# Cross-attention on one core: 25 key chunks of 128 and two keys in a resident sample, in place of 26 chunks of about 123

## The chip, the core and the metric

The kernel runs on one core of a Trainium2 chip. A core has TensorE (matrix products, with weight loads listed apart), VectorE, ScalarE and GpSimd (elementwise work and reductions), and SyncE, which here only issues DMA transfers. The metric is the device time of one execution in microseconds (us).

## The reference

All numbers are 32-bit floats. 4096 query rows x and 3202 context rows, each 512 wide, are layer-normalized. Eight heads of 64 attend from the queries to the context; the result is projected, added to x, normalized again, and fed to a small recurrence of 64 states. Cut to what matters here:

```python
x = layernorm(builder_state, g1, beta1)          # 4096 x 512
base_n = layernorm(base_state, g1, beta1)        # 3202 x 512
q, k, v = heads(x, Wq, bq), heads(base_n, Wk, bk), heads(base_n, Wv, bv)
attn = softmax(q @ k.T / sqrt(64))               # 8 heads, 4096 x 3202
x = residual + (attn @ v) @ W_o.T + b_o
U = (layernorm(x, g2, beta2) @ W_in.T + b_in) @ Bmat
# s = silu(s @ A.T) + u_t over 4096 steps; out = x + states @ Cmat + mod
```

## The kernel before

*Preparation* (up to `prep.close()`, L586). The 3202 context rows are split into `NCH` = 26 chunks of 122 to 124 rows (`keys(c)`, L50; `key0(c)`, L56, is where a chunk begins). A chunk is loaded (`load_chunk`), normalized (`norm_chunk`: statistics on VectorE, factors on GpSimd, scaling on ScalarE) and transposed (`turn_chunk`). Its values are four products into `pv` (L542), copied on ScalarE to `vs` and stored to `vd` in DRAM (L552). After every fourth chunk, and after the last, the keys of that group of chunks are projected for each of four pairs of heads (`pk`, L568), biased on ScalarE into `ks` (L576), and stored to `kd` in DRAM (L581). Side work, such as the first queries, is threaded between. Within this part each engine takes its instructions in the order in which they are written.

*Attention.* The queries are taken in `NQB` = 8 groups of 512. A unit is one group Q, one pair of heads hp, and one half of the group (`QU` = 256 queries): 64 units. A unit goes through `NDC` = 13 steps; a step c is a pair of blocks, that is of chunks, of keys. Per step:

- `scores` (L615): for two blocks b, two halves of a block's keys and two heads a, a product with 256 moving columns. Contraction is over the 64 values of a head, so each product uses one quarter (64 by 64) of TensorE's array, and the four of one block use all quarters. In the trace a product of 32-bit floats is two instructions, so a step's scores are 16.
- `weights` (L670): ScalarE takes the exponential of the step's scores, 1024 a partition, less a shift.
- `product` (L694): the exponentials times the values, again quarter by quarter, 16 instructions, summed over the unit in PSUM (`po`).
- `add` (L678): the exponentials are summed elementwise into `acc`, on VectorE, in steps 2, 6 and 10 on GpSimd (`POOL_SUMS`). At a unit's end GpSimd folds the two blocks (`fold`, L683) and TensorE sums over the keys (`sums`, L708) for the denominator, which ScalarE copies out (L734) into `rd` and a scratch tile.

The shift is common to the two halves of a (Q, hp). Before its first unit a *sample* of scores is made (`sample`, L632): the first 64 keys of block 0, from the loaded tile `kts[Q, hp, 0]`, with all 512 queries. VectorE takes the maximum (`maximum`, L644), TensorE spreads it (`spread`, L651), and VectorE reduces it to the shift (`base`, L662). The sample lies in one of the two PSUM buffers that scores use (ring `s`).

Keys and values of a step are loaded from DRAM by `load_k` (L953) and `load_v` (L961), issued on SyncE's queue 10 and 6 steps ahead of the scores that they are for, once for both halves of a (Q, hp) except in the last group of queries.

*What sets the order.* The class `Plan` (L60) is a planner: each piece of work is given an engine, an assumed cost in ns, the pieces it comes after, a due time, and rings of buffers that it takes or gives back. `order()` runs a list schedule with these costs, earliest due first, and the pieces are then emitted in that order, which is fixed for each engine. Products are due `LAG` = 4 steps after their scores. Kinds of pieces in quarters and of whole-array pieces are kept together, as a change between them is assumed to cost time. The pieces of a unit are added in `unit` (L1302), those of its end in `finish` (L725).

*The end.* `drain` (L1358) adds the recurrence in two sweeps over 16 rows in parallel columns, the last query rows, and the output. A general version of the attention (`attend`, L1458) runs only where checks on the device find that the quick one doesn't hold.

Of the kernel before, what the change touches and what calls it, by code (L numbers as in the profile page):

```python
# [20 lines left out]
P = 128  # L21
NC = H // P
NCH = 26
CK = 124
NDC = NCH // 2
GC = 4
# [15 lines left out]

RISE = 2.0**60
# [6 lines left out]
def keys(c):  # L50


    return {0: CK, 1: CK, 2: CK - 2, NDC - 1: CK}.get(c // 2, CK - 1)


def key0(c):  # L56
    return sum(keys(k) for k in range(c))
# [104 lines left out]
def xattn_ssm_kernel(  # L162
# [41 lines left out]
    shifts = const.tile([P, NQB * NC], F32, name="shifts")  # L204
    neg_half = const.tile([P, 1], F32, name="neg_half")
# [308 lines left out]
    with tc.manual_schedule():  # L514
# [20 lines left out]
        for c in range(NCH):  # L535
# [5 lines left out]
            for i in range(NC):  # L541
# [8 lines left out]
            vs = cin.tile([CK, NC, P], F32, tag="vs", name=f"vs_{c}")  # L550
            nc.scalar.copy(vs[:n], pv[:n, :H])
            nc.sync.dma_start(  # L552
                vd[:, c // 2, :n, c % 2, :].rearrange("h p d -> p h d"), vs[:n]
            )
# [10 lines left out]
            for hp in range(NC):  # L565
# [13 lines left out]
                for b in range(g * GC, c + 1, 2):  # L579
                    m, k = 2 * keys(b), key0(b) - key0(g * GC)  # L580
# [26 lines left out]
    def scores(w, c):  # L607

        n, q = keys(2 * c), w["q"]
        s = ps_s.tile([P, 2, 2, QU], F32, tag="s", name=f"s_{w['name']}_{c}")  # L610
        for b in range(2):
            for k0, k1 in ((0, HD), (HD, n)):
                for a in range(2):
                    r = slice(a * HD, (a + 1) * HD)
                    nc.tensor.matmul(  # L615
                        s[k0:k1, a, b, :],
                        kts[(*w["at"][:2], c)][r, b * n + k0 : b * n + k1],
# [7 lines left out]
    def sample(w):  # L625
# [3 lines left out]
        for part in range(2):  # L629
            for a in range(2):  # L630
                r = slice(a * HD, (a + 1) * HD)
                nc.tensor.matmul(  # L632
                    s[part * HD : (part + 1) * HD, a, 0, :],
                    kts[Q, hp, 0][r, :HD],
                    qt[Q, hp][r, part * QU : (part + 1) * QU],
# [29 lines left out]

    def weights(w, c):

        n = keys(2 * c)
        t = w["s"][c] = sp_.tile([CK, 2, 2, QU], F32, tag="s", name=f"p_{w['name']}_{c}")
        nc.scalar.activation(t[:n], w["ps"][c][:n], AF.Exp, bias=w["shift"][:n])  # L670

    def add(w, c, engine):

        n, t = keys(2 * c), w["s"][c]
# [3 lines left out]
        engine.tensor_tensor(w["acc"][:n], t[:n], before[:n], ALU.add)  # L678
# [6 lines left out]
    def product(w, c):  # L685


        n, t = keys(2 * c), w["s"][c]
        if c == 0:
            w["po"] = ps_o.tile([P, 2, 2 * QU], F32, tag="o", name=f"po_{w['name']}")  # L690
        for b in range(2):
            for a in range(2):
                for k, (k0, k1) in enumerate(((0, HD), (HD, n))):
                    nc.tensor.matmul(  # L694
                        w["po"][a * HD : (a + 1) * HD, k, :QU],
                        vts[(*w["at"][:2], c)][k0:k1, b, a * HD : (a + 1) * HD],
# [1004 lines left out]
```

## Time and profile before

| | us |
|---|---|
| median of the runs shown (three, 2144.7 to 2152.58) | 2149.72 |
| profiled execution, device time | 2149.4 |
| its span, first to last instruction | 2147.6 |
| TensorE busy (matmul) | 2081.9 |
| TensorE busy (weight loads, beside the matmuls) | 1528.4 |
| ScalarE busy | 1245.4 |
| VectorE busy | 1086.0 |
| GpSimd busy | 759.9 |
| mean granted clock of TensorE, share of full | 0.990 |

In the views of the profile PE is TensorE's matmuls, PEld its weight loads, DVE VectorE, ACT ScalarE, POOL GpSimd, SPq SyncE's queue. A group's row gives line, engine, operation, out<-in, the shape and the count, then its busy time and the mean duration of one in ns, then the idle time of the engine just before its instructions and what ended it. Busy times count time in which at least one instruction of the group ran, so matmuls that overlap in quarters are not counted four times. A row of the chain of waits or of the timeline gives start and length in us.

### The profile page before, as it was taken

How to read it: one execution, taken by the hardware profiler on the slowest of the kernel's cores; microseconds unless marked ns; L12 is line 12 of the kernel's file. 1: busy time of each engine (PE TensorE's matmuls, PEld its weight loads, DVE VectorE, ACT ScalarE, POOL GpSimd, SP SyncE). 2: the span in 40 equal slices, each digit the busy share in tenths (PEclk: the TensorE clock that was granted, in tenths of full speed). 3: DMA queues.
4: the chain of work that ended last, by engine and by line, in shares of the span. 5: the costliest groups of instructions: out<-in, count | busy, mean ns of one | idle time of the engine just before them, and what ended most of it. 6: DMA issues, size and time to landing. Idle time of an engine off the chain costs nothing.

```text
span 2147.6 us, 67311 instructions
## 1 busy us (share of the span) xinstructions
PE 2081.9 (97%) x29822; PEld 1528.4 (71%) x29822; DVE 1086.0 (51%) x1227; ACT 1245.4 (58%) x1734; POOL 759.9 (35%) x622
## 2 busy tenths in 40 slices
PE   6998999999999999999999999999999999999997
PEld 2444587787788777887778777877787777767754
DVE  2121056555555546464556455555555464645555
ACT  2132267656665677557656676566656675566642
POOL 1111034334432444234423443344424442344313
PEclk9999999999999999999999999999999999999997
DMA  3332332222221222122212322222222221444464
GB/s 118 122 122 93 91 97 80 64 74 75 80 75 57 74 74 82 53 65 93 78 59 78 93 78 63 73 77 81 74 57 74 74 82 53 125 130 133 132 191 159
DMA packets 178117, 190.73 MB, mean 89 GB/s; under 512 B 14252, under 2 KB 151256, under 8 KB 177818
## 3 DMA queue, kind: packets, MB, share of 16 engines
q1 hardware_dynamic: 173270, 178.67, 27.4%
q10 hardware_dynamic: 4548, 7.67, 1.2%
q8 instruction: 237, 3.88, 0.8%
q14 instruction: 62, 0.51, 0.1%
HBM read 156.40 MB, written 29.89 MB: 87 GB/s over the span
## 4 chain that ended last, share of the span: by engine, by line
PE 79%; ACT 6%; DVE 5%; DMA 4%; POOL 4%; issue 1%; SPq 1%; ACTq 0%; POOLq 0%; DVEq 0%
PE s L615 29%; PE po L694 27%; PE pq L301 5%; PE pv L542 4%; PE pk L568 3%; DVE acc L678 3%; PE pa L874 3%; ACT p L670 2%; DMA x<-in_x_dram 2%; POOL acc L678 2%; PE pu L921 1%; PE pd L708 1%; POOL rstd_x L795 1%; PE tp_x L271 1%; ACT xh_x L799 1%
## 5 line engine op out<-in xcount | busy, mean ns | idle before, releaser
L670 ACT ACTIVATE p<-s,shifts 123x1024 f32<-123x1024 f32 (+2 forms) x832 | 922.3, 1115 | 371.3 <-PE s L615 368.8
L694 PE MATMUL po<-p,v 64*64 64x256 f32 (+3 forms) x13312 | 887.1, 376 | 0.2 <-DVE o L723 0.2
L615 PE MATMUL s<-q,k 64*64 64x256 f32 (+3 forms) x13312 | 885.2, 377 | 0.8 <-ACT p L670 0.2
L678 DVE TENSOR_TENSOR acc<-p,acc 123x1024 f32<-123x1024 f32 (+2 forms) x515 | 644.2, 1251 | 447.1 <-POOL acc L678 230.3
L678 POOL TENSOR_TENSOR acc<-p,acc 122x1024 f32<-122x1024 f32 x189 | 447.2, 2366 | 851.4 <-ACT p L670 496.1
L694 PEld LDWEIGHTS po<-p,v 64*64 64x64 f32 (+3 forms) x13312 | 586.1, 133 | 137.9 <-issue 13.0
L615 PEld LDWEIGHTS s<-q,k 64*64 64x64 f32 (+3 forms) x13312 | 571.0, 131 | 157.3 <-issue 15.6
L678 DVE TENSOR_TENSOR acc<-p,p 124x1024 f32<-124x1024 f32 x64 | 86.0, 1343 | 147.7 <-ACT p L670 147.7
L683 POOL TENSOR_TENSOR acc<-acc 124x512 f32<-124x512 f32 x64 | 81.5, 1274 | 132.2 <-DVE acc L678 109.4
L301 PE MATMUL pq<-xn,wq 128*128 128x256 f32 x512 | 117.4, 384 | 0.0
L742 DVE RECIPROCAL rd<-rd 128x256 f32<-128x256 f32 (+1 forms) x65 | 111.7, 1720 | 0.4
L301 PEld LDWEIGHTS pq<-xn,wq 128*128 128x128 f32 x512 | 95.2, 190 | 21.7 <-issue 9.7
L874 PE MATMUL pa<-wo,o 128*128 128x512 f32 x240 | 108.8, 601 | 0.0
L542 PE MATMUL pv<-wv,ct 128*123 128x512 f32 (+2 forms) x208 | 99.9, 626 | 0.0
L568 PE MATMUL pk<-ct,wk 128*128 128x492 f32 (+3 forms) x224 | 89.1, 550 | 0.0
L576 ACT ACTIVATE ks<-pk,bias 128x492 f32<-128x492 f32 (+3 forms) x28 | 18.0, 642 | 118.8 <-PE pk L568 59.8
L723 DVE TENSOR_TENSOR o<-po,o 128x256 f32<-128x256 f32 x64 | 26.9, 420 | 112.7 <-ACT o L719 112.5
L874 PEld LDWEIGHTS pa<-wo,o 128*128 128x128 f32 x240 | 43.7, 190 | 51.3 <-issue 50.8
L310 ACT ACTIVATE q<-pq,bias 128x512 f32<-128x512 f32 x32 | 22.0, 686 | 95.8 <-PE pq L301 95.8
L782 ACT ACTIVATE xh_y<-x 128x512 f32<-128x512 f32 x30 | 18.8, 627 | 98.3 <-DVE x L884 98.3
L512 DVE COPY ct<-tp_c 128x492 f32<-128x492 f32 (+2 forms) x13 | 8.7, 671 | 126.3 <-PE tp_c L271 126.3
L542 PEld LDWEIGHTS pv<-wv,ct 128*123 128x123 f32 (+2 forms) x208 | 39.3, 197 | 46.7 <-issue 45.8
(190 smaller groups left out, 1308.0 us busy)
## 6 DMA issues: line engine op xcount, KB each, us to landing
k<-kd SPq DMA_DIRECT2D x324, 123.0 KB
v<-vd SPq DMA_DIRECT2D x324, 123.0 KB
k<-kd SPq DMA_DIRECT2D x108, 124.0 KB
v<-vd SPq DMA_DIRECT2D x108, 124.0 KB
xr<-in_x_dram SPq DMA_DIRECT2D x32, 256.0 KB
x1d<-xr SPq DMA_DIRECT2D x32, 256.0 KB
x<-in_x_dram SPq DMA_DIRECT2D x28, 256.0 KB
cx<-in_ctx_dram SPq DMA_DIRECT2D x18, 246.0 KB
```

The costliest lines, as they stand in the source:

```text
L301: nc.tensor.matmul(pq[:, half * QU : (half + 1) * QU], wq[:, i, hp * P : (hp + 1) * P], xns[half][:, i, :], start=(i == 0), stop=(i == NC ...
L310: nc.scalar.activation(t, pq, AF.Identity, bias=bias[:, hp : hp + 1], scale=HD**-0.5)
L542: nc.tensor.matmul(pv[:n, :H], ct[:, i, o : o + n], wv[:, i, :], start=(i == 0), stop=(i == NC - 1),)
L568: nc.tensor.matmul(pk[:, :n_g], wk[:, i, hp * P : (hp + 1) * P], ct[:, i, :n_g], start=(i == 0), stop=(i == NC - 1),)
L615: nc.tensor.matmul(s[k0:k1, a, b, :], kts[(*w["at"][:2], c)][r, b * n + k0 : b * n + k1], q[r], start=True, stop=True, skip_group_check=True,)
L670: nc.scalar.activation(t[:n], w["ps"][c][:n], AF.Exp, bias=w["shift"][:n])
L678: engine.tensor_tensor(w["acc"][:n], t[:n], before[:n], ALU.add)
L683: nc.gpsimd.tensor_tensor(acc[:, :, 0, :], acc[:, :, 0, :], acc[:, :, 1, :], ALU.add)
L694: nc.tensor.matmul(w["po"][a * HD : (a + 1) * HD, k, :QU], vts[(*w["at"][:2], c)][k0:k1, b, a * HD : (a + 1) * HD], t[k0:k1, a, b, :], sta ...
L723: nc.vector.tensor_tensor(o, w["po"][:, 1, :QU], o, ALU.add)
L742: nc.vector.reciprocal(w["rd"][:, part], w["rd"][:, part])
L874: nc.tensor.matmul(v["pa"], o_t[Q, c, t // 2][:, t % 2 * P : (t % 2 + 1) * P], wo[:, c, :], start=(c == 0), stop=(c == NC - 1),)
```

## The change

The 3202 keys become 25 full chunks of 128 (`CK` = 128) and a 26th chunk of the two keys that are left (`REST` = 2).

- In the preparation the 26th chunk's values go to `vx`, an SBUF tile that is zero elsewhere, on partitions 0 and 1, and by a small DMA also on partitions 64 and 65. GpSimd copies keys into `kx`, 64 for each pair of heads: the two keys left over first, then the first 62 keys. `vd` gets no values of the 26th chunk.
- Step 12 of a unit has one block: scores, weights, products and addition are of half size there.
- The sample is made from `kx`, so its scores hold those of the two keys left over. A new piece `extra` on ScalarE takes the exponential of all the sample's scores, once the shift is known, into a tile of a ring of 4; it gives back the sample's PSUM buffer, which `base` gave back before. Sample columns are ordered so that query half t of each unit stands on partitions t * 64 on.
- `rest`, a new piece on VectorE, adds the two keys' exponentials to `acc` in each unit: two additions on two partitions and 2 x 128 columns, after the unit's addition 1 and before 2.
- Ahead of step 12's products come four products of 128 columns, exponentials of the sample times `vx`, into `po`. As `vx` is zero elsewhere, only the two keys count.
- The sample no longer waits for the step of the unit before that issued its keys' load.
- The copy of the second denominator goes back to its own PSUM tile, not to a scratch tile.
- The planner's costs are given anew: scores 864 (before 860) and 432 for the half step, products 864 and 650, weights 1061 and 630, additions on VectorE 1300 and 700, `extra` 640, `rest` 700.

```diff
-CK = 124
+CK = 128
+REST = S2 - (NCH - 1) * CK
 def keys(c):
-    return {0: CK, 1: CK, 2: CK - 2, NDC - 1: CK}.get(c // 2, CK - 1)
+    return CK if c < NCH - 1 else REST
+def blocks(c):
+    return 2 if c < NDC - 1 else 1
...
+    kx = const.tile([P, NC, HD], F32, name="kx")
+    vx = const.tile([P, H], F32, name="vx")
+    nc.gpsimd.memset(vx, 0.0)
...
+            if c < NCH - 1:
+                vs = cin.tile([CK, NC, P], F32, tag="vs", name=f"vs_{c}")
+                nc.scalar.copy(vs, pv)
+                nc.sync.dma_start(vd[:, c // 2, :, c % 2, :].rearrange("h p d -> p h d"), vs)
+            else:
+                nc.scalar.copy(vx[:n], pv[:n])
+                nc.sync.dma_start(vx[HD : HD + n], vx[:n])
...
+                if g == 0:
+                    nc.gpsimd.tensor_copy(kx[:, hp, REST:], ks[:, : HD - REST])
+                elif c == NCH - 1:
+                    nc.gpsimd.tensor_copy(kx[:, hp, :REST], ks[:, CK : CK + REST])
...
     def scores(w, c):
-        for b in range(2):
-            for k0, k1 in ((0, HD), (HD, n)):
+        for b in range(blocks(c)):
+            for k0 in (0, HD):
...
     def sample(w):
-        for part in range(2):
+        q = qt[Q, hp].rearrange("p (h t j) -> p t h j", h=2, t=2)
+        for t in range(2):
             for a in range(2):
                 nc.tensor.matmul(
-                    s[part * HD : (part + 1) * HD, a, 0, :],
-                    kts[Q, hp, 0][r, :HD],
-                    qt[Q, hp][r, part * QU : (part + 1) * QU],
+                    s[t * HD : (t + 1) * HD, a, 0, :],
+                    kx[r, hp, :],
+                    q[r, t],
...
+    def extra(w):
+        t = extras[w["at"][:2]] = accp.tile([P, 2, 2, P], F32, tag="extra", name=f"x_{w['name']}", bufs=4)
+        nc.scalar.activation(
+            t, w["sample"][:, :, 0, :].rearrange("p a (h j) -> p a h j", h=2), AF.Exp, bias=w["shift"]
+        )
+
+    def rest(w):
+        t = extras[w["at"][:2]][:, :, w["at"][2], :]
+        for k in range(2):
+            r, to = slice(k * HD, k * HD + REST), w["acc"][:, :, 0, k * P : (k + 1) * P]
+            nc.vector.tensor_tensor(to[r], t[r], to[r], ALU.add)
...
     def product(w, c):
+        if c == NDC - 1:
+            for a in range(2):
+                for k in range(2):
+                    r = slice(k * HD, (k + 1) * HD)
+                    nc.tensor.matmul(
+                        w["po"][a * HD : (a + 1) * HD, k, k * P : (k + 1) * P],
+                        vx[r, hp * P + a * HD : hp * P + (a + 1) * HD],
+                        extras[Q, hp][r, a, half, :],
+                        start=False, stop=False, skip_group_check=True,
+                    )
-        for b in range(2):
+        for b in range(blocks(c)):
...
-            to = w["rd"] if k == 0 else op.tile([P, QU], F32, tag="junk", ...)
+            to = w["pd"][k][:, :QU] if k else w["rd"]
...
-            free = [("scores", i - 1, NDC - AHEAD_K)] if i else []
-            plan.add(("sample", i), "PE", 440, partial(sample, w), q + free, d, ["s"], ...)
-            plan.add(("base", i), "DVE", 280, partial(base, w), [("spread", i)], d + 1000, [],
+            plan.add(("sample", i), "PE", 440, partial(sample, w), q, d, ["s"], ...)
+            plan.add(("base", i), "DVE", 280, partial(base, w), [("spread", i)], d + 1000)
+            plan.add(("extra", i), "ACT", 640, partial(extra, w), [("base", i)], d + 1000, ["extra"],
                      [("s", ("sample", i))])
...
+            if c == 1:
+                plan.add(("rest", i), "DVE", 700, partial(rest, w), [("add", i, 1), ("extra", first)],
+                         d + 1300, [], [("extra", ("extra", first))])
```

Left out above: the loads of `load_k` and `load_v`, which take one block in step 12; the additions, which take half there; the planner's other costs; and `attend`, which follows the new layout.

More of the change, by code (lines that the diff above doesn't have):

```diff
@@ L50, in keys @@
 def keys(c):
-    return {0: CK, 1: CK, 2: CK - 2, NDC - 1: CK}.get(c // 2, CK - 1)
+    return CK if c < NCH - 1 else REST
+def blocks(c):
+    return 2 if c < NDC - 1 else 1
 def key0(c):
-    return sum(keys(k) for k in range(c))
+    return c * CK
 class Plan:
@@ L677, in add @@
             w["acc"] = accp.tile([CK, 2, 2, QU], F32, tag="acc", name=f"acc_{w['name']}")
-        engine.tensor_tensor(w["acc"][:n], t[:n], before[:n], ALU.add)
+        engine.tensor_tensor(
+            w["acc"][:, :, :nb, :], t[:, :, :nb, :], before[:, :, :nb, :], ALU.add
+        )
     def fold(w):
@@ L706, in sums @@
         for a in range(2):
[L707 removed]
+            for k, (k0, k1) in enumerate(((0, HD), (HD, P))):
                 nc.tensor.matmul(
@@ L732, in denominators @@
                 w["rd"] = op.tile([P, QU], F32, tag="rd", name=f"rd_{name}", bufs=2)
-            to = w["rd"] if k == 0 else op.tile([P, QU], F32, tag="junk", name=f"junk_{name}", bufs=1)
+            to = w["pd"][k][:, :QU] if k else w["rd"]
             nc.scalar.activation(
@@ L951, in load_k @@
             t = kp.tile([P, 2 * CK], F32, tag="k", name=f"k_{Q}_{hp}_{half}_{c}")
-            n = 2 * keys(2 * c)
+            n = blocks(c) * CK
             nc.sync.dma_start(t[:, :n], kd[hp, c, :, :n])
@@ L1323, in unit @@
             d = max(s0 - REF, 0) * STEP
-            free = [("scores", i - 1, NDC - AHEAD_K)] if i else []
-            plan.add(("sample", i), "PE", 440, partial(sample, w), q + free, d, ["s"],
+            plan.add(("sample", i), "PE", 440, partial(sample, w), q, d, ["s"],
                      [("q", ("heads", Q, hp))], "quarters")
@@ L1336, in unit @@
             old = [("product", *divmod(g, NDC))] if g >= 0 else []
-            plan.add(("scores", i, c), "PE", 860, partial(scores_, c), q + old, d, ["s"],
+            part = blocks(c) / 2
+            plan.add(("scores", i, c), "PE", 864 * part, partial(scores_, c), q + old, d, ["s"],
                      [("q", ("heads", Q, hp))], "quarters")
-            plan.add(("weights", i, c), "ACT", 1061, partial(weights, w, c),
+            plan.add(("weights", i, c), "ACT", 200 + 861 * part, partial(weights, w, c),
                      [("scores", i, c), ("base", first)], d + 1000, ["p"],
@@ L1343, in unit @@
             p = ("p", ("weights", i, c))
-            plan.add(("product", i, c), "PE", 860, partial(product_, c),
-                     [("weights", i, c)] + ([("product", i, c - 1)] if c else []),
-                     d + 1000, [] if c else ["o"], [p], "quarters")
+            more, gives = [], [p]
+            if c == NDC - 1:
+                more, gives = [("extra", first)], [p, ("extra", ("extra", first))]
+            plan.add(("product", i, c), "PE", 864 if part == 1 else 650, partial(product_, c),
+                     [("weights", i, c)] + ([("product", i, c - 1)] if c else []) + more,
+                     d + 1000, [] if c else ["o"], gives, "quarters")
             if c:
                 dve = w["last"] or c not in POOL_SUMS
-                plan.add(("add", i, c), "DVE" if dve else "POOL", 1300 if dve else 2382,
+                before = {1: ("weights", i, 0), 2: ("rest", i)}.get(c, ("add", i, c - 1))
+                plan.add(("add", i, c), "DVE" if dve else "POOL", (100 + 1200 * part) if dve else 2382,
                          partial(add, w, c, nc.vector if dve else nc.gpsimd),
-                         [("weights", i, c), ("weights" if c == 1 else "add", i, c - 1)], d + 1200,
+                         [("weights", i, c), before], d + 1200,
                          ["acc"] if c == 1 else [],
                          [p] + ([("p", ("weights", i, 0))] if c == 1 else []))
+            if c == 1:
+                plan.add(("rest", i), "DVE", 700, partial(rest, w), [("add", i, 1), ("extra", first)],
+                         d + 1300, [], [("extra", ("extra", first))])
         d += 2000
```

84 lines of the change are left out of this document (44 added, 40 removed).

## The prediction

> **What bounds the kernel now.** I read the page first, then the busy time by stage, then the chain of waits inside one stretch of the loop, then what TensorE itself waited for. The page:
>
> ```profile
> span 2147.6 us, 67311 instructions
> PE 2081.9 (97%) x29822; PEld 1528.4 (71%) x29822; DVE 1086.0 (51%) x1227; ACT 1245.4 (58%) x1734; POOL 759.9 (35%) x622
> ...
> L615 PE MATMUL s<-q,k 64*64 64x256 f32 (+3 forms) x13312 | 885.2, 377 | 0.8 <-ACT p L670 0.2
> ```
>
> No engine but TensorE is near its limit, yet a busy PE need not be a PE at its peak, so the stages come next (columns: stretch, length, busy time and instructions of each engine, granted clock, DMA):
>
> ```profile
> 0.00:259.20 259.20, 226.40 (x661) 107.40 (x661) 46.71 (x110) 64.84 (x103) 33.14 (x98) 0.98 0.34 107
> 259.20:2063.00 1803.80, 1791.18 (x28857) 1381.46 (x28858) 997.47 (x993) 1159.83 (x1561) 700.94 (x489) 1.00 0.28 82
> 2063.00:2147.60 84.60, 64.33 (x308) 39.51 (x306) 41.85 (x125) 20.69 (x71) 25.85 (x36) 0.81 0.55 170
> ```
>
> The attention loop is 1803.8 of 2147.6 us, and TensorE is busy for 1791.2 of it at a granted clock of 1.00. Whether that time is also full is seen in a stretch of pure loop, and in the chain of waits around one sample:
>
> ```profile
> 709.94:728.93 18.99, 18.99 (x356) 16.07 (x352) 13.31 (x12) 12.42 (x13) 7.88 (x4) 1.00 0.12 31
> ```
>
> ```profile
> 458.80 0.86 PE po L694 x16
> 459.67 0.43 PE sm L632 x8
> 460.10 0.87 PE po L694 x16
> 460.97 0.86 PE s L615 x16
> 461.83 0.84 PE po L694 x15
> 462.67 0.09 PE sm L651 x5
> 462.75 0.05 PE po L694
> 462.80 0.01 PE sm L651
> 462.81 0.86 PE po L694 x14
> 463.68 1.73 PE s L615 x32
> ```
>
> In 18.99 us the sequencer issued 352 weight loads, each with its matmul: 22 pieces of 16 (the scores or the products of one pair of blocks), 0.863 us a piece. The chain steps from one piece to the next with no gap and no other engine between them. The waits of TensorE over the loop (waiter, releaser, us, times, longest) say the same, and those of ScalarE say who leads:
>
> ```profile
> PEld s L615 <- ACT p L670: 12.5, 32, 0.6
> PE tp_x L271 <- ACT xh_x L799: 10.4, 16, 1.2
> ```
>
> ```profile
> ACT p L670 <- PE s L615: 368.8, 555, 2.0
> ```
>
> ScalarE waits 369 us for scores, TensorE hardly ever for anything. So the loop goes at the rate at which TensorE can issue, and matmul time taken out of it comes off the end, unless something new stalls it.
>
> **The change, part by part.** The loop has 64 units (8 groups of 512 queries, 4 pairs of heads, 2 halves) of 13 steps. The diff makes step 12 one block instead of two.
>
> *Matmuls removed.* Their cost follows the moving columns, 256 queries, and not the keys: the page's group holds forms with 58, 59, 60 and 64 keys, and keys set only the stationary side, so blocks of 128 keys cost what blocks of 123 did. That half a piece costs half shows at the sample: eight instructions of 256 columns, 0.43 us. Per unit half of a scores piece and half of a products piece go: 2 x 0.4315 = 0.863 us; over 64 units 55.2 us.
>
> *Matmuls added.* Four products of 128 columns per unit, eight instructions over the four quadrants. No row has this form. By columns they cost half of the sample's 0.43, 0.216 us. The nearest rows on both sides are the sample (0.43) and the spreading of the maximum just after it, eight instructions of 64 columns, 0.09 + 0.05 + 0.01 = 0.15 us with a product between. I take 0.216, since the short row shows that one instruction per 19 ns can go through and mine need only one per 27 ns: 64 x 0.216 = 13.8 us, bounds 9.6 and 27.5.
>
> A rule of the Trainium skill speaks against this. TensorE: Matmul & The Clock Gate, Back-to-back issue gap, states that in a stream of weight loads and matmuls a matmul of 128 columns takes about 81 ns, more than its columns alone. By it 512 instructions would cost 41.5 us, an estimate, and the change would keep 13.7 us. The row of 64 columns, with 19 ns each, does not agree for quadrants that run side by side; no row here shows 128 columns in quadrants.
>
> *The sample moves.* It multiplies the resident keys (two left over and the first 62) with the same 512 queries in eight instructions: 0.43 us as before. What is new is that its score buffer, one of two, is given back by an exponential on ScalarE and not by the VectorE reduction before it. Here is that time in the trace:
>
> ```profile
> 461.95 1.11 ACT L670 ACTIVATE p<-s,shifts 123x1024 f32<-123x1024 f32 x1 [1.98 <-PE s L615]
> 464.60 2.12 ACT L670 ACTIVATE p<-s,shifts 123x1024 f32<-123x1024 f32 x2 [1.54 <-PE s L615]
> ```
>
> ```profile
> 462.87 0.29 DVE L662 TENSOR_REDUCE shifts<-sm 128x1 f32<-128x128 f32 x1
> ```
>
> ```profile
> 264.40 0.69 ACT L310 ACTIVATE q<-pq,bias 128x512 f32<-128x512 f32 x1 [6.20 <-PE pq L301]
> ```
>
> The reduction ends at 463.16. ScalarE is idle from 463.06 to 464.60, so an exponential of 512 elements (0.69 us by the row of that size, and some 0.15 us, an estimate, for the two hand-overs) fits there, and the buffer is free at about 464.0 and not 463.2. The chain's two scores pieces begin at 463.68 and 464.54; the first has the other buffer, freed at 463.06, and the second needs this one with half a microsecond to spare. Queued behind the exponential are the next weights; they wait for scores anyway. So the hold costs nothing where the order falls like this. Where ScalarE is in the middle of weights it may cost up to the whole 0.85 us, 32 x 0.85 = 27.2 us. Below nothing is excluded: the buffer is never held shorter. I take 0.1 us each, 3 us, near the end that the trace shows.
>
> *ScalarE and VectorE.* The rows for them, of the groups by form:
>
> ```profile
> L670 ACT ACTIVATE p<-s,shifts 123x1024 f32<-123x1024 f32 x576 | 638.6, 1115 | 269.6 <-PE s L615 267.3
> L678 DVE TENSOR_TENSOR acc<-p,acc 123x1024 f32<-123x1024 f32 x450 | 564.5, 1254 | 437.5 <-POOL acc L678 230.3 <-ACT p L670 188.4 <-POOL nm_y L796 3.4
> L678 POOL TENSOR_TENSOR acc<-p,acc 123x1024 f32<-123x1024 f32 x126 | 298.4, 2368 | 636.2 <-ACT p L670 343.4 <-DVE acc L678 292.8
> L749 DVE TENSOR_TENSOR o<-o,rd 128x256 f32<-128x256 f32 x63 | 56.9, 903 | 1.5
> L739 DVE TENSOR_TENSOR rd<-pd,rd 128x256 f32<-128x256 f32 x64 | 26.8, 420 | 8.5 <-ACT junk L734 8.5
> ```
>
> ScalarE loses about half of 64 exponentials (64 x 0.5 = 32 us) and gains 32 x 0.69 = 22: a little lighter. VectorE loses half of 64 additions (64 x 0.6 = 38 us) and gains 128 small ones on two partitions, 256 elements, between 0.42 and 0.90 us each by the last two rows: 54 to 115 us, so it stands at 1100 to 1165 us, below 56% of the span. These additions lie between the second addition of a unit and the third, on GpSimd; the whole chain of a unit is then 9 x 1.25 + 3 x 2.37 - 0.6 + 1.8 = 19.6 us at most, against 1803.8 / 64 = 28 us for a unit of the loop now, and 27.6 after. Cover enough: 0. The second denominator copy writes PSUM instead of a scratch tile, same size: 0.
>
> *DMA and queues.* Each pair of heads still issues its 13 loads of keys and 13 of values, same queue, same bytes in all (the DMA share in the loop is 0.28). The sample no longer waits for a step that issued its keys: 0.
>
> *Preparation.* There are still 26 chunks; the last holds two keys and its value products cost what a full one does. Key products follow the columns:
>
> ```profile
> 230.05 13.37 PE L568 MATMUL pk<-ct,wk 128*128 128x492 f32 x32
> ...
> 250.12 6.86 PE L568 MATMUL pk<-ct,wk 128*128 128x248 f32 x32
> ```
>
> From these, 6.5 us for 244 columns: six groups of 512 instead of some 492 add 6 x 0.53 = 3.2 us, and the last group of 130 instead of 248 saves up to 3.1 us. I take +1. GpSimd gets eight copies of up to 62 columns behind the key projections; in the first group the normalization of a later chunk queues behind one:
>
> ```profile
> 63.03 0.67 ACT L576 ACTIVATE ks<-pk,bias 128x496 f32<-128x496 f32 x1 [7.21 <-DMA kd<-ks]
> 63.60 0.80 ACT L255 ACTIVATE xh_c<-cx,nmr_c,rstd_c 123x512 f32<-123x512 f32 x1
> ...
> 70.45 0.58 PE L271 MATMUL tp_c<-ident,xh_c 123*128 123x123 f32 x4
> ```
>
> It would be some 2 us late, and the transposes that need it come at 70.45, about 6 us after its end; were that cover gone, the 2 us would be paid once. Cost 0.
>
> *Tail.* It is a serial scan with its own chain; only the last addition shrinks, by 0.6 us: 0.
>
> **Sum.** -55.2 + 13.8 + 3 + 1 = -37.4 us. The profiled execution took 2149.4 us, its span 2147.6, and the median of the runs shown is 2149.72, so both scales agree to 0.3 us. Forecast: 2149.4 - 37.4 = 2112 us, 1.7% faster.
>
> **Rivals.**
>
> *The held buffer stalls TensorE.* If the second scores piece finds the sample's buffer taken in every one of 32 samples, with no products ready to fill in, 27.2 us replace the 3: 2136 us. For it: two buffers only, and 12.5 us of waits for weights already, in 32 places. Against it: products stand four steps behind scores by the order's due times, and TensorE filled the present 3.8 us hold with them.
>
> *The short products do not overlap.* Their columns stream for only 0.216 us, and the weights of eight instructions must come in within it. One weight load takes 133 ns:
>
> ```profile
> L694 PEld LDWEIGHTS po<-p,v 64*64 64x64 f32 x6656 | 488.1, 133 | 137.9 <-issue 13.0 <-DVE o L723 2.9 <-DMA k<-kd 0.8
> ...
> 563.69 1.02 PE pu L921 x8
> ```
>
> Mild form: only two of them run at a time, 8 x 133 / 2 = 0.53 us a unit, 34.0 us instead of 13.8, and the time is 2132 us. Slow form, and the rival that ends slower: the short products, at the head of step 12's products, go one after another as the eight 128-column matmuls of the state inputs do (the second row, 1.02 us): 65.3 us instead of 13.8, and the time is 2163 us. From 0.80 us a unit on, (55.2 - 4) / 64, the change loses. Against both: eight 64-column instructions in the same four quadrants took 0.15 us, with weights of the same size. By the rule of the Trainium skill above it would be 2140 us, an estimate.
>
> *The change doesn't do what it says.* The work written for step 12 shrinks, but the order is planned anew, and a step of half length may leave TensorE waiting at each unit's end for most of the half-size exponential (0.69 us by the row above, say 0.6) with nothing else ready: 64 x 0.6 = 38 us would be given back and 2150 us remain. For it: the planner counts costs and not what really happens. Against it: the next unit's scores and products four steps behind are ready at that place, as in all of the loop now.
>
> **How the numbers follow.** Forecast 0.79; held buffer 0.10; short products 0.03 in the mild form and 0.02 in the slow one; time given back 0.06. About 0.5%, 11 us, is what a measurement of this kernel can tell from no change, so faster means below 2139 us. Forecast, held buffer and mild form are faster, 0.92, less 0.02 for a hold with a whole exponential of weights queued in front (another 1.1 us in part of the samples), which would end within 0.5%. With 0.04 of the time given back that makes 0.06 for the same; its other 0.02 and the slow form are 0.04 for slower. The range: with short products at 0.15 us and nothing for buffer and preparation the sum gives 2104; upward, short products at 0.43 give 2126, and three quarters of the held buffer's stall 2130. So 2103 to 2130.
>
> **What would show it.** In the profile after: 12800 instead of 13312 instructions in the scores' group, eight short product instructions per unit taking about 0.22 us in the chain; the loop some 38 us shorter, preparation and tail within 2 us of 259 and 85. Wrong would be the buffer's step if scores' waits for weights grow from 12.5 us by tens; the short products' step if the chain gives them 0.4 us or more; the cover on VectorE if sums or products wait for additions; the whole, if the loop loses less than 20 us.

## The result and the profile after

| | before | after |
|---|---|---|
| median, us | 2148.77 (2144.7 to 2152.58) | 2094.67 (2093.36 to 2095.41) |
| profiled execution, us | 2149.4 | 2095.41 |
| its span, us | 2147.6 | 2093.2 |

The ratio is 0.9748, with a 95% interval of 0.9729 to 0.9767: 54 us or 2.5% faster. The direction was right, but the time is 17 us below the forecast of 2112 and 8 us below the lower end of the range. The page after:

```profile
span 2093.2 us, 66347 instructions
PE 2039.0 (97%) x29310; PEld 1342.8 (64%) x29310; DVE 1102.0 (53%) x1355; ACT 1241.2 (59%) x1766; POOL 756.1 (36%) x631
...
L741 PE MATMUL po<-p,v 64*64 64x256 f32 x12800 | 838.8, 377 | 13.6 <-DVE o L770 13.6
...
L631 PE MATMUL s<-q,k 64*64 64x256 f32 x12800 | 837.2, 377 | 3.1 <-ACT p L701 1.8
```

TensorE is busy for the same 97%, so the page alone does not say where the gain came from. The busy time by stage does, if the stages hold the same work. The prediction's loop ended with the last product, and by that end it went from 1803.8 to 1776.0 us. But in the kernel after, the order that is planned anew puts the last half step's products behind output projections (`py`) and the first steps of the recurrence (`z`), over 8 us after the products ahead of them:

```profile
1998.11 4.50 PE L741 MATMUL po<-p,v 64*64 64x256 f32 x80
2002.43 0.61 PE L755 MATMUL pd<-acc,ones 64*64 64x256 f32 x8
2002.97 1.98 PE L1211 MATMUL py<-wo,o 128*128 128x512 f32 x4
...
2010.70 0.45 PE L729 MATMUL po<-x,vx 64*64 64x128 f32 x8
```

Before, the last products follow one another. So I end the loop with the last scores. To there the kernels differ by 512 matmul instructions, 1016 taken out and 504 put in. The loop and what comes behind it, before and then after (columns as in the prediction: stretch, length, PE, PEld, DVE, ACT, POOL, granted clock, DMA share, GB/s):

```profile
259.20:2057.10 1797.90, 1785.28 (x28756) 1377.02 (x28760) 995.06 (x987) 1157.65 (x1555) 697.62 (x486) 1.00 0.27 82
2057.10:2147.60 90.50, 70.23 (x413) 43.95 (x404) 44.26 (x131) 22.86 (x76) 29.17 (x38) 0.82 0.57 177
```

```profile
0.00:235.60 235.60, 221.05 (x662) 103.45 (x662) 46.02 (x110) 65.89 (x103) 34.96 (x107) 1.00 0.38 117
235.60:1998.30 1762.70, 1743.62 (x28244) 1194.53 (x28248) 1011.45 (x1115) 1152.78 (x1587) 691.80 (x487) 1.00 0.29 84
1998.30:2093.20 94.90, 74.38 (x412) 44.82 (x404) 44.55 (x131) 22.53 (x76) 29.32 (x38) 0.79 0.51 152
```

| stage | before | after | difference | forecast |
|---|---|---|---|---|
| preparation | 259.2 | 235.6 | -23.6 | +1 |
| loop, to the last scores | 1797.9 | 1762.7 | -35.2 | -38.4 |
| tail, from the last scores | 90.5 | 94.9 | +4.4 | 0 |

Two steps of the forecast failed. The preparation, where nothing was to happen, gave 23.6 of the 54 us. In the loop, TensorE's busy time fell by 41.7 us, and 41.4 were forecast for its matmuls; but its idle time rose from 12.6 to 19.1 us, and behind this stand two waits that moved in opposite directions; their rows come further down.

The tail is 85 to 90 us long in those of the sixteen kernels here that were granted a clock of 0.89 or more in it, and 90 to 96 at 0.83 or less, with nearly the same work. So I compare stages, and the loop above all. How well the loop repeats differs: in after and the two kernels below whose loop is the same it took 1762.3 to 1762.7 us; before took 1797.9 and a kernel with the same loop 1801.7. Differences of a few us are no reading between kernels of another order.

The signs that the prediction named: the scores' group has 12800 instructions, as told, and the short products take 0.22 us in the chain, as told. The chain around them:

```profile
320.53 0.22 PE po L729 x8
320.75 0.43 PE po L741 x8
```

The held sample buffer costs nothing that shows: the scores' waits for weights went from 12.5 us to 8.8. New is the second row, the wait that the prediction named as the sign against its step on VectorE; it was 0.2 us before. Gone is most of a wait that the prediction shows at 10.4 us, for the normalized queries (`xh_x`): the third row (waits of TensorE and of its weight loads: waiter, releaser, us, times, longest):

```profile
PEld s L631 <- ACT p L701: 8.8, 17, 1.2
PE po L741 <- DVE o L770: 13.6, 14, 1.7
PE tp_x L281 <- ACT xh_x L846: 1.3, 6, 0.3
```

So a wait of 13.4 us that was forecast at nothing came in, and 9.1 us that nobody counted went out. Why they went is not shown; it is luck that the loop ends within 3.2 us of its forecast.

### The profile page after: what moved, and what is told of

Same layout as the page of the kernel before. It is cut to its first block, busy times and chain, and to the rows that moved or that the text cites. A ratio compares the mean times of both kernels' runs of the same rounds, so it can differ in the third digit from the quotient of the medians.

```text
span 2093.2 us, 66347 instructions
## 1 busy us (share of the span) xinstructions
PE 2039.0 (97%) x29310; PEld 1342.8 (64%) x29310; DVE 1102.0 (53%) x1355; ACT 1241.2 (59%) x1766; POOL 756.1 (36%) x631
## 4 chain that ended last, share of the span: by engine, by line
PE 81%; DVE 7%; ACT 5%; POOL 5%; issue 2%; DMA 0%; POOLq 0%; ACTq 0%; DVEq 0%
PE po L741 27%; PE s L631 26%; PE pq L311 6%; PE pa L921 5%; PE pv L552 4%; DVE acc L709 4%; PE pk L580 4%; ACT p L701 3%; POOL acc L709 3%; PE pu L968 1%; POOL rstd_x L842 1%; PE tp_x L281 1%; PE pd L755 1%; DVE acc L695 1%; POOL rstd_x L841 1%
## 5 line engine op out<-in xcount | busy, mean ns | idle before, releaser
L701 ACT ACTIVATE p<-s,shifts 128x1024 f32<-128x1024 f32 (+1 forms) x832 | 894.7, 1082 | 334.2 <-PE s L631 322.3
L741 PE MATMUL po<-p,v 64*64 64x256 f32 x12800 | 838.8, 377 | 13.6 <-DVE o L770 13.6
L709 DVE TENSOR_TENSOR acc<-p,acc 128x1024 f32<-128x1024 f32 (+1 forms) x515 | 611.3, 1187 | 445.4 <-POOL acc L709 297.4
L631 PE MATMUL s<-q,k 64*64 64x256 f32 x12800 | 837.2, 377 | 3.1 <-ACT p L701 1.8
L709 POOL TENSOR_TENSOR acc<-p,acc 128x1024 f32<-128x1024 f32 x189 | 448.0, 2371 | 819.6 <-DVE acc L709 403.7
L631 PEld LDWEIGHTS s<-q,k 64*64 64x64 f32 x12800 | 481.2, 133 | 223.3 <-issue 24.0
L741 PEld LDWEIGHTS po<-p,v 64*64 64x64 f32 x12800 | 479.7, 133 | 214.0 <-DVE o L770 20.0
L709 DVE TENSOR_TENSOR acc<-p,p 128x1024 f32<-128x1024 f32 x64 | 88.5, 1383 | 125.5 <-ACT p L701 119.3
L716 POOL TENSOR_TENSOR acc<-acc 128x512 f32<-128x512 f32 x64 | 81.8, 1277 | 113.6 <-DVE acc L709 113.6
L552 PE MATMUL pv<-wv,ct 128*128 128x512 f32 (+1 forms) x208 | 95.4, 602 | 0.0
L580 PE MATMUL pk<-ct,wk 128*128 128x512 f32 (+1 forms) x224 | 89.3, 551 | 0.0
L829 ACT ACTIVATE xh_y<-x 128x512 f32<-128x512 f32 x30 | 18.8, 627 | 113.0 <-DVE x L931 113.0
L770 DVE TENSOR_TENSOR o<-po,o 128x256 f32<-128x256 f32 x64 | 26.9, 421 | 83.9 <-ACT o L766 83.7
```

The source lines that it names most:

```text
L552: nc.tensor.matmul(pv[:n, :H], ct[:, i, o : o + n], wv[:, i, :], start=(i == 0), stop=(i == NC - 1),)
L580: nc.tensor.matmul(pk[:, :n_g], wk[:, i, hp * P : (hp + 1) * P], ct[:, i, :n_g], start=(i == 0), stop=(i == NC - 1),)
L631: nc.tensor.matmul(s[k0 : k0 + HD, a, b, :], kts[(*w["at"][:2], c)][r, b * CK + k0 : b * CK + k0 + HD], q[r], start=True, stop=True, skip_ ...
L701: nc.scalar.activation(t[:, :, :nb, :], w["ps"][c][:, :, :nb, :], AF.Exp, bias=w["shift"])
L709: engine.tensor_tensor(w["acc"][:, :, :nb, :], t[:, :, :nb, :], before[:, :, :nb, :], ALU.add)
L716: nc.gpsimd.tensor_tensor(acc[:, :, 0, :], acc[:, :, 0, :], acc[:, :, 1, :], ALU.add)
```

## The experiments

### The preparation

In the profile after, the preparation's chain is nearly all TensorE, behind one weight load of 5.49 us; before, it waited for two transfers of the chunks, 24.1 us in all. These, a load and a store of values, in the chain of waits before, and then the first chunk's statistics in VectorE's timelines of before and of after:

```profile
1.63 13.12 DMA cx<-in_ctx_dram
...
94.47 10.98 DMA vd<-vs
```

```profile
6.89 0.69 DVE L234 BATCH_NORM_STATS2 st_c<-cx 124x6 f32<-124x512 f32 x1 [5.83 <-DMA cx<-in_ctx_dram]
```

```profile
3.49 0.69 DVE L244 BATCH_NORM_STATS2 st_c<-cx 128x6 f32<-128x512 f32 x1 [2.43 <-DMA cx<-in_ctx_dram]
```

The first chunk's statistics start 3.4 us sooner although the chunk is larger. The theory: a transfer of 128 rows goes faster than one of 122 to 124. The rival: the new layout of the preparation (two rows in the last chunk, other group sizes, the copies on GpSimd) does it. Four kernels cut the chunk's transfers by rows, on both sides:

```diff
+def parts(n):
+    return [slice(0, 123), slice(123, n)] if n > 123 else [slice(0, n)]   # rows64: 64 for 123
-            nc.sync.dma_start(xt[:n], ctx_in[key0(c) : key0(c) + n, :])
+            for r in parts(n):
+                nc.sync.dma_start(xt[r], ctx_in[key0(c) + r.start : key0(c) + r.stop, :])
```

and the same for the store of `vs` to `vd`. In the kernel after, *rows123* makes 123 rows and 5 of each full chunk, *rows64* twice 64, so both issue the same number of transfers. In the kernel before, *rows112* makes 112 rows and the 10 to 12 that are left, and *rows112v* does that in the loop's loads of values too.

> The changed kernel with each context load and each value store of the preparation cut into 123 and 5 rows, two transfers in place of one. Theory (rows): a transfer whose row count isn't a multiple of 16 is carried by few of the 16 DMA engines, so 122 to 124 rows were slow before and 128 are not; then the preparation, 235.6 us after the change, goes back towards 259 us, and the total rises by 15 to 24 us to 2110 to 2119 us. Rival (tiling of the preparation): the 23.6 us come from another place, such as the last chunk of two keys or the order on the engines; then the total is 2095 to 2100 us.

> The changed kernel with the same transfers cut into 64 and 64 rows: as many transfers as in the cut of 123 and 5, but both multiples of 16. Theory (rows): 2095 to 2100 us, preparation 235 to 240 us. Rival (the second issue on the queue costs, not the row count): the same time as the cut of 123 and 5.

> The kernel before with each context load and value store of the preparation cut into 112 rows (7 x 16) and the 10 to 12 left. Theory (rows): the preparation falls from 259.2 to 236 to 245 us without anything of the change, the total to 2125 to 2137 us. Rival (tiling of the preparation): 2147 to 2152 us.

> As the one before it, and the loads of values in the loop cut in the same way. Theory (rows): the loop hides its loads, so no more than 2 us below the one before it. Rival (the loop too gained from 128 rows): 5 to 15 us below it.

| kernel | median | ratio to before | preparation | loop, to the last scores |
|---|---|---|---|---|
| after, rows 123 and 5 | 2110.28 | 0.9805 [0.9774, 0.9835] | 256.6 | 1762.3 |
| after, rows 64 and 64 | 2095.41 | 0.9729 [0.9703, 0.9755] | 239.1 | 1762.5 |
| before, rows 112 and 10 to 12 | 2129.75 | 0.9903 [0.9874, 0.9931] | 239.5 | 1801.7 |
| before, the same and the loop's values | 2129.54 | 0.9884 [0.9856, 0.9913] | 239.4 | 1797.1 |

The stages of rows123, rows64 (both after) and rows112 (before):

```profile
0.00:256.60 256.60, 223.39 (x658) 103.57 (x658) 47.22 (x110) 64.61 (x103) 34.82 (x106) 0.99 0.34 108
```

```profile
0.00:239.10 239.10, 221.21 (x658) 103.42 (x658) 46.48 (x110) 65.89 (x103) 34.97 (x106) 1.00 0.41 116
```

```profile
0.00:239.50 239.50, 220.74 (x662) 106.02 (x663) 47.03 (x110) 65.59 (x103) 33.53 (x98) 1.00 0.41 116
```

The rival falls. With rows of 123 the new layout is back at 256.6 us; with rows of 112 the old one comes down to 239.5, and the kernel before gains 1.0 to 1.2% without any change of its chunks. TensorE's work in the stage is the same in these, 221 to 223 us. Splitting alone costs 3.5 us (239.1 against 235.6). Loads and stores were cut together; what each gave was not tried apart. That the loop's loads of values were cut as well changed nothing (2129.54 and 2129.75): 6 steps ahead they are hidden whatever they take, as the prediction had it.

What the row count does is seen in the DMA view of the first 40 us, in slices of 1 us: busy share of the 16 DMA engines in tenths, and GB/s. Before, then after with rows 123 and 5, then after:

```profile
DMA  0147899999723332222211111112222221111122
GB/s 0 9 58 105 266 227 295 389 391 291 227 97 104 104 100 100 100 102 98 73 51 51 53 72 74 76 76 74 76 84 95 95 72 49 53 49 44 48 63 89
```

```profile
DMA  0139799999321122222112212221121111211222
GB/s 0 16 35 156 260 285 301 328 375 373 141 78 74 74 80 78 81 77 78 76 74 80 62 76 78 80 78 76 78 78 76 76 76 74 78 76 67 65 70 69
```

```profile
DMA  0179999999706995000097196000000591620009
GB/s 0 37 227 363 414 389 373 399 391 398 170 0 119 350 389 191 0 0 0 16 269 240 32 278 215 0 0 0 0 0 0 174 289 62 183 80 15 0 18 143
```

In the first 10 us the large weight loads run beside the chunks and each of the three kernels comes to a peak between 370 and 415 GB/s. Behind them the chunks are alone. After, each comes as a short burst near the same rate and the engines rest between. Before, the stream crawls at three levels, 97 to 104, 72 to 76 and 49 to 53 GB/s, and never rests; with 123 rows the level is 74 to 81 nearly throughout. These are 4, 3 and 2 sixteenths of 390: 98, 73 and 49. So 124 rows went over four engines, 123 over three and 122 over two. This is read from the rates, not from a record of each engine. The Trainium skill has the rule: DMA: Bandwidth & Descriptors, Why a DMA increments its semaphore by 16 and not by 1, says that a copy is spread over the largest number of engines, at most 16, that divides the count of its outermost rows on both sides. It gives 4, 3 and 2 for 124, 123 and 122, and 16 for 128, 112 and 64; the levels agree with it. By it the step could have been priced in advance.

### The loop: which part of the change cost how much

TensorE waits 13.6 us in the loop for VectorE's copy. The theory: the small additions of the left-over keys (`rest`) make VectorE late for this copy, which frees the products' accumulator. The rivals: the short products cost more than 13.8 us; the held buffer costs; the halved step does not give its 55.2 us. The first kernels take parts out or double them. In *without* and *noshort* the planner's cost of step 12's products falls from 650 to 432 as well, and in *extra2* that of the exponential doubles. The expectations count the loop to its last product, which makes it some 13 us longer than in the table, alike in all six kernels:

```diff
# without: no exponential of the sample, no small additions, no short products
# (the two left-over keys are left out); base gives the buffer back as before
-            plan.add(("extra", i), "ACT", 640, ...)
-            plan.add(("rest", i), "DVE", 700, ...)
-        if c == NDC - 1:  # the four short products
# norest: the small additions alone (the two keys are left out of the denominators)
-            plan.add(("rest", i), "DVE", 700, ...)
# noshort: the short products alone (the two keys are left out of the products)
-        if c == NDC - 1:
# short2: the short products twice, the second time with weights of zero
+            for left in (lambda r, a: vx[r, ...], lambda r, a: vz[r]):
# extra2: the exponential of the sample twice
+        for _ in range(2):
```

> The changed kernel without what joins the two keys left over: no exponential of the sample, no additions of two partitions, no short products (so the two keys are left out of the attention; the buffer of the sample is given back by the VectorE reduction). Theory (additions): 13.8 us of short products go, and with the small additions the waits of the first products of a unit for the copying out of the unit before (13.6 us after the change) go as well: 2068 to 2076 us. Rival (half step): those waits come from the shorter step 12 and stay, 2079 to 2083 us.

> The changed kernel without the small additions (the two keys are left out of the denominators). Without all that joins the two keys the loop was 1751.1 us, with it 1776.0. Theory (additions): of these 24.9 us the short products are 14.1 (0.22 us a set in the chain) and the small additions, through the order that they force, the other 10.8; so the loop is 1764 to 1767 us and the total 2082 to 2086 us. Rival (the order planned anew falls as it falls): the parts don't add up, and the total lies anywhere from 2072 to 2097 us.

> The changed kernel without the short products (the two keys are left out of the products, and stay in the denominators). Theory (additions): 14.1 us less, loop 1761 to 1763 us, total 2079 to 2083 us. Rival (the order planned anew falls as it falls): as with the products twice, where the loop took 6.8 us more for 14.1 us of work, the loop changes by another amount, 5 to 20 us, and the parts don't add up to 24.9.

> The changed kernel with every set of four short products issued twice, the second time with a tile of zeros as weights. Theory (the short products stream at the rate of their columns): 64 x 0.216 = 13.8 us more, 2106 to 2111 us. Rival (short products wait for their weights): 0.43 to 1.02 us a unit, 27 to 65 us more, 2122 to 2160 us.

> The changed kernel with the exponential of the sample done twice, so that the score buffer is held some 0.69 us longer in 32 places and the planner knows it. Theory (the hold is covered by products that are ready): 2094 to 2099 us. Rival (held buffer): up to 32 x 0.69 = 22 us more, 2105 to 2117 us.

| kernel | median | ratio to before | loop, to the last scores | against after | waits of products for the copy |
|---|---|---|---|---|---|
| after | 2094.67 | 0.9748 [0.9729, 0.9767] | 1762.7 | | 13.6 |
| without | 2068.09 | 0.9609 [0.9587, 0.9632] | 1738.0 | -24.7 | 5.2 |
| no small additions | 2080.99 | 0.9671 [0.9650, 0.9691] | 1749.4 | -13.3 | 2.2 |
| no short products | 2080.16 | 0.9678 [0.9655, 0.9701] | 1754.6 | -8.1 | 15.9 |
| short products twice | 2099.33 | 0.9760 [0.9735, 0.9785] | 1769.3 | +6.6 | 9.0 |
| exponential twice | 2092.42 | 0.9720 [0.9693, 0.9746] | 1763.4 | +0.7 | 14.4 |

The stage of the loop in *without* and in *no small additions*:

```profile
236.60:1974.60 1738.00, 1727.66 (x27740) 1205.85 (x27744) 962.72 (x987) 1133.18 (x1555) 688.75 (x487) 1.00 0.29 85
```

```profile
236.10:1985.50 1749.40, 1742.34 (x28244) 1221.60 (x28248) 963.62 (x987) 1153.41 (x1587) 685.90 (x487) 1.00 0.29 85
```

Read down the table:

- The halved step alone takes the loop down by 59.9 us (1797.9 - 1738.0), 57.6 of them busy time of TensorE. Forecast for it were 55.2. That rival falls.
- Short products and exponential together, with no small additions in the way, cost 11.4 us (1749.4 - 1738.0). Forecast were 13.8 and 3.
- The exponential twice moves the loop by 0.7 us. The hold is covered.
- The small additions, forecast at nothing, cost 13.3 us (1762.7 - 1749.4), and the waits for the copy fall by 11.4 without them. The 2.2 to 5.2 us of these waits that stay, against 0.2 before, come with the rest of the change or with the order planned anew. Without the small additions the loop stands at -48.5 us, and the forecast was -38.4.
- The short products twice: a set of 16 takes 0.44 to 0.46 us in the chain, so 14 us of work came in, and the loop grew by only 6.6, since TensorE's idle time fell by 6.4, 4.6 of them waits for the copy. The 2099.33 us are below the 2106 to 2111 that were expected. Taken out, the short products gave 8.1 us, less than expected too: TensorE was busy 12.5 us less and idle 4.4 us more. An instruction's price and its worth in the end differ where TensorE waits anyway.

### How the small additions stall TensorE

They work on two partitions and 256 elements, 0.44 us each, 56 us in all, half of what the prediction allowed at most. The groups of VectorE and the one of GpSimd (by form, columns as on the page):

```profile
L695 DVE TENSOR_TENSOR acc<-x,acc 2x256 f32<-2x256 f32 x128 | 56.0, 438 | 3.0
```

```profile
L709 POOL TENSOR_TENSOR acc<-p,acc 128x1024 f32<-128x1024 f32 x189 | 448.0, 2371 | 819.6 <-DVE acc L709 403.7 <-ACT p L701 292.6 <-DVE acc L695 100.7
```

GpSimd now waits 100.7 us for them. One of the longest of TensorE's stalls, in the timelines of VectorE, GpSimd and TensorE:

```profile
471.16 2.30 DVE L709 TENSOR_TENSOR acc<-p,p 128x1024 f32<-128x1024 f32 x1
473.50 0.84 DVE L695 TENSOR_TENSOR acc<-x,acc 2x256 f32<-2x256 f32 x2
476.91 2.28 DVE L709 TENSOR_TENSOR acc<-p,acc 128x1024 f32<-128x1024 f32 x1 [2.57 <-POOL acc L709]
479.11 0.41 DVE L770 TENSOR_TENSOR o<-po,o 128x256 f32<-128x256 f32 x1
```

```profile
471.11 1.28 POOL L716 TENSOR_TENSOR acc<-acc 128x512 f32<-128x512 f32 x1 [2.13 <-DVE acc L709]
474.51 2.37 POOL L709 TENSOR_TENSOR acc<-p,acc 128x1024 f32<-128x1024 f32 x1 [2.12 <-DVE acc L695]
476.85 1.27 POOL L916 TENSOR_TENSOR xr<-xr,rowb 128x512 f32<-128x512 f32 x1
```

```profile
479.58 1.09 PE L741 MATMUL po<-p,v 64*64 64x256 f32 x16 [1.65 <-DVE o L770]
```

Two small additions; behind them GpSimd's addition of step 2; behind that VectorE's addition of step 3, for which VectorE stands still for 2.57 us; and in VectorE's queue behind this one the copy (`o`, L770) that frees the products' accumulator. The copy's own input was ready at 476.63, when ScalarE's half of it ended. The next unit's first products wait for it for 1.65 us. All 14 such waits of the loop have this row before them: a VectorE addition that waited 2.54 to 2.58 us for GpSimd, and then the copy. They come in two sizes, eight of 0.41 to 0.61 us and six of 1.62 to 1.65. In all six the addition took 2.27 to 2.28 us while GpSimd ran an addition of its own (L916), as in the timeline above; in seven of the eight it took 1.23, as at 370.81, with GpSimd idle.

Five kernels move that knot, with all the work kept in each:

```diff
# rest3: the small additions after addition 3, addition 4 waits for them
-                before = {1: ("weights", i, 0), 2: ("rest", i)}.get(c, ("add", i, c - 1))
+                before = {1: ("weights", i, 0), 4: ("rest", i)}.get(c, ("add", i, c - 1))
# pool3 (after) and before-pool3 (before): GpSimd's additions one step later
-    POOL_SUMS = (2, 6, 10)
+    POOL_SUMS = (3, 7, 11)
# rest12: the small additions at the unit's end, the fold waits for them
-        plan.add(("fold", i), "POOL", 1250, partial(fold, w), [("add", i, NDC - 1)], d + 500)
+        plan.add(("fold", i), "POOL", 1250, partial(fold, w), [("rest", i)], d + 500)
# both: rest12 and pool3 together
```

> The changed kernel with the small additions one step later by two: after a unit's addition 3 and before 4, both on VectorE, and not before addition 2 on GpSimd. Theory (additions): GpSimd starts its addition some 0.85 us earlier, VectorE's queue reaches the copying out of the products earlier, and the waits of the first products shrink from 13.6 to below 6 us: 2083 to 2090 us. Rival (half step): 2093 to 2097 us.

> The changed kernel with GpSimd's additions in steps 3, 7 and 11 in place of 2, 6 and 10, so that VectorE waits for GpSimd one step later than where it copies out the products of the unit before. Theory (the copying out queues behind an addition that waits for GpSimd): the waits of the first products fall from 13.6 to below 4 us, the loop by 8 to 13 us, the total to 2080 to 2088 us. Rival (the order planned anew): no gain, 2092 to 2100 us.

> The kernel before with GpSimd's additions in steps 3, 7 and 11 in place of 2, 6 and 10. Theory (the small additions made the wait): the first products waited only 0.2 us before, so the loop of 1803.5 us changes by less than 5 us and the total stays at 2144 to 2155 us. Rival (the place of GpSimd's additions is worth as much without the change): loop 1786 to 1795 us, total 2130 to 2140 us.

> The changed kernel with the small additions at the end of a unit's additions, before the folding. Theory (additions): GpSimd's first addition is not held up, waits of the first products below 6 us, loop 3 to 11 us less, total 2083 to 2091 us. Rival (the order planned anew): as with the additions after step 3, 2093 to 2098 us.

> The changed kernel with GpSimd's additions in steps 3, 7 and 11 and the small additions at the end of a unit's additions. Theory (the wait is the only loss of the loop beside the matmuls): it is already gone with steps 3, 7 and 11, so nothing more comes off, 2070 to 2079 us. Rival (the small additions cost by themselves): 5 us or more below the run with steps 3, 7 and 11.

| kernel | median | ratio to before | loop, to the last scores | tail from there | waits of products for the copy |
|---|---|---|---|---|---|
| rest3 | 2095.51 | 0.9743 [0.9717, 0.9768] | 1767.8 | 89.5 | 5.3 |
| pool3 | 2075.85 | 0.9651 [0.9632, 0.9670] | 1744.8 | 85.9 | 0.2 |
| before-pool3 | 2150.36 | 0.9996 [0.9981, 1.0011] | 1800.4 | 91.6 | |
| rest12 | 2089.03 | 0.9718 [0.9695, 0.9740] | 1760.7 | 87.1 | 9.7 |
| both | 2088.89 | 0.9710 [0.9686, 0.9734] | 1759.8 | 95.5 | 0.9 |

In rest3, rest12 and both the last products follow one another as in the kernel before, so here too only the stretch to the last scores compares.

*pool3* bears the mechanism out: the same instructions on every engine, only GpSimd's additions one step later, so that VectorE goes straight on after the small additions. The waits for the copy are gone and the loop ends 17.9 us sooner:

```profile
236.20:1981.00 1744.80, 1738.91 (x28244) 1217.97 (x28248) 993.25 (x1115) 1152.72 (x1587) 704.20 (x487) 1.00 0.29 85
```

TensorE's idle time fell from 19.1 to 5.9 us, about what the waits for the copy fell by; the other 4.7 us are busy time, and why these went is open. At 0.9651 it beats both kernels. The 18.8 us between its median and that of after are the loop's 17.9, but for 1 us; its profiled execution alone had a short tail, 85.9 us at a clock of 0.93, and took 2068.67 us where its other executions took 2075.75 to 2076.69. In the kernel before, the same move is worth nothing (0.9996; the loop is 2.5 us longer), so it is no gain by itself: the places 2, 6 and 10 were as good as 3, 7 and 11 until the small additions stood ahead of the first of them.

*rest3* was expected to give most of this and did not; its loop is 5.1 us longer than that of after. The waits for the copy fell by 8.3 us, but others rose in their place, so that TensorE's idle time is the same (18.9 us), and its busy time is 5.3 us more:

```profile
PEld s L631 <- ACT p L701: 19.9, 39, 1.0
...
PE pu L968 <- ACT xn L960: 5.2, 6, 0.9
```

*Both* was expected at 2070 to 2079 us and missed this too. Its two edits took 2.0 and 17.9 us off the loop by themselves and 2.9 together, with the first products no longer waiting, but these:

```profile
PE tp_x L281 <- ACT xh_x L846: 10.2, 13, 1.2
...
PE pd L755 <- POOL acc L716: 4.7, 7, 0.7
```

So to remove this wait is not enough. Each edit has the order of all pieces planned anew, and where it then falls is not told by the piece that was moved. In TensorE's timeline the changes between quarter pieces and whole-array pieces, up to the last scores, went from 182 before to 206 after, and to 202 to 210 in the other kernels made from it. What these cost by themselves was not tried apart.

## Why the prediction was right and wrong, step by step

- *What bounds the kernel:* right for the loop. Time of matmuls taken out came off the end in full: 59.9 us with the halved step alone, 55.2 forecast.
- *Matmuls added:* right. 0.22 us a set in the chain, 0.216 forecast. The mild and the slow form of the rival are out, and so is, for quadrants, the 81 ns of TensorE: Matmul & The Clock Gate, Back-to-back issue gap, in the Trainium skill: eight instructions in 0.22 us are 27 ns each.
- *The sample moves:* the hold is covered. 3 us were allowed; the exponential twice moved the loop by 0.7 us, and this is one profile a side, so about 0 to 1 us is what can be said.
- *ScalarE and VectorE, "Cover enough: 0":* failed, 13.3 us by *no small additions*. The sum of busy time was right, even generous (56 us against 54 to 115). Wrong was the comparison: a unit's additions, 19.6 us, against a unit of the loop, 28 us, says that VectorE keeps up on the mean. It doesn't say what stands behind a late addition in VectorE's queue. What it had to name is the copy that frees the products' accumulator, for which TensorE waits.
- *DMA and queues:* right for the loop, which is what it spoke of.
- *Preparation, "I take +1":* failed by 24.6 us, and this is what put the time below the range. It counted chunks, columns of matmuls and copies on GpSimd, and left out the transfers of the chunks themselves and the stores of their values, which change from 122 to 124 rows to 128. The bound was in sight: the stage's row shows TensorE busy for 226.4 of 259.2 us at a DMA share of 0.34, so 33 us were waits of TensorE that the prediction did not follow to their cause. The prediction read the chain of waits only inside the loop.
- *Tail, 0:* +4.4 us from the last scores on, at a granted clock of 0.79 against 0.82, within what the tail does from kernel to kernel.
- *The loop's sum, -38.4:* -35.2, near by luck. The 13.3 us of the small additions were missing from it, short products and exponential cost 11.4 and not 16.8, and the halved step gave 4.7 us more than its 55.2; the waits for normalized queries, which the prediction shows and leaves as they are, went from 10.4 to 1.3 us.
- *Rival "the change doesn't do what it says":* no step leaves TensorE waiting at every unit's end. But its doubt about the order planned anew was the right kind of doubt, and a smaller one of that kind came true 14 times.

Together: 24.6 us of gain that was missed in the preparation, less 3.2 that the loop kept and 4.4 of the tail, make the 17 us by which the forecast was too high.

## What to carry to other kernels

Read the chain of waits in every stage that the change touches, however small its share, and count each transfer by its rows as well as its bytes: 5 rows more made a chunk's load faster, and padding or splitting to a row count that 16 divides may be worth more than the arithmetic that it was not meant for. When work is added to an engine with room, follow that engine's queue to the next piece for which the bounding engine waits; room on the mean is no cover. When one such knot is found, try moving the other engine's work as well as the new work, and measure each, since every move shifts the rest of the order. And end a stage with an instruction that closes the same work in both kernels: by the last product, which had slid into the tail, the loop seemed to miss its forecast by 10.6 us, and by the last scores it missed by 3.2.

## What the runs showed of the hardware

- Transfers of 122, 123 and 124 rows ran at some 50, 75 and 100 GB/s where those of 128 came in bursts of up to 389, at the same width; the preparation was 256.6 us with 123 and 5 rows and 239.1 with 64 and 64.
- VectorE's additions do not run beside GpSimd's: the one that starts later waits. In the loop after, 432 additions of 1024 elements that met no GpSimd instruction took 1.22 us each (1.16 to 1.23). The 30 that met GpSimd's addition of L916 or its fold (L716), begun ahead of them, took 2.12 us on average, with 1.04 us of overlap. So VectorE lost nearly all of the time that they shared. In two cases VectorE's addition began 0.17 to 0.18 us ahead of L916's; it took 1.29 to 1.30 us, and L916's 2.25 instead of 1.26 to 1.29. Beside GpSimd's one-element operation of L841 (41 cases) VectorE took 1.23. The Trainium skill names such a contention, for VectorE instructions with two inputs in the on-chip memory (GPSIMD Engine Reference, Key points); these rows agree and give it a size. The prediction's sum of a unit's additions, by means, could not show it.
- From the last scores to the end the sixteen kernels took 85 to 96 us for nearly the same work, with granted clocks of 0.93 to 0.79. On a time of 2090 us that is up to 0.5%, more than some of the effects sought.
